# Two token tiles' last 64 inner values abreast on TensorE's row halves, in the down products of a shared FFN

## The chip, the cores and the metric

The kernel runs on one core of a Trainium2 chip. A core has five engines with queues of their own, which meet at semaphores: TensorE (matrix products; in the profile PE, its weight loads PEld), VectorE (DVE), ScalarE (ACT), GpSimd (POOL) and SyncE (SP, which here issues most DMA transfers). Products land in PSUM; everything else lives in SBUF or, off the core, in HBM. The metric is the device time of one execution in microseconds, and smaller is better.

## The reference, cut to what matters

The kernel computes one layer: cross attention, then a mixture of 64 experts with six of them per token, and a shared FFN that every token passes. The change touches the shared FFN. B, S, D = 4, 512, 512 give 2048 tokens; the shared FFN has FS = 704 inner values.

```python
def _shared_swiglu(x, wg, wu, wd):
    return jax.nn.silu(x @ wg.T) * (x @ wu.T) @ wd.T
...
g = jnp.einsum('ecd,efd->ecf', buf, w_gate)
u = jnp.einsum('ecd,efd->ecf', buf, w_up)
eo = jnp.einsum('ecf,edf->ecd', jax.nn.silu(g) * u, w_down)
gathered = eo[se, pos_c] * (sw * valid.astype(sw.dtype))[:, None]
y = jnp.zeros_like(x).at[st].add(gathered).reshape(B, S, D)
return y + _shared_swiglu(hidden_states, sh_gate, sh_up, sh_down)
```

## The kernel before

All arrays are float32. The tokens form 16 tiles of 128 (`TB` = 4 tiles in each of the 4 batches), and `acc` holds for each tile the residual to which everything is added.

The order of the work: attention over all tiles with the router, which scatters token numbers into lists in HBM (`list_d`, line 477); near its end, the shared FFN of batch 0, interleaved with the last tiles' routing and with `plan()`, which loads the lists back (line 491), sums them on VectorE (line 504), spreads them (508), turns them on TensorE (515) and writes `lists` (518). Then come the gate and up products of batch 1, whose down products wait; the loop over 64 experts (gather tokens, line 834; products, lines 871 to 927; results to `eo_d`, lines 952 and 956); and the tail: the down products of batch 1, the whole shared FFN of batches 2 and 3, and, interleaved with them, 96 gathers of expert results by GpSimd (line 1017), each followed by a weighted sum into `acc` on VectorE (line 1028). A tile whose last sum is done is written out (line 1005).

The order on each engine is written out by hand inside `manual_schedule`: an engine runs its instructions in the order in which the Python code issues them, and generators with `yield` interleave the parts. In `shared(b, get)`:

- The inner values come in six chunks, `FSC`: five of 128 and one of 64. For each, line 132 makes the gate and up products of all 512 tokens, line 143 the silu on ScalarE and line 144 the multiplication into `hid` on VectorE. In the last chunk gate and up share one product: gate in rows 0 to 63 of the PSUM bank, up in rows 64 to 127.
- The down products (lines 146 to 153): for each tile m one PSUM bank from `get.pd()`, six products accumulated in it (the last with 64 rows), and one addition into `acc` (line 152). A float32 product shows in the trace as two passes, each with a weight load of its own.
- Where PSUM comes from: for batch 0, `Here.pd` takes a tile of the pool `ps_s` (line 758), which has two buffers, shared with `Here.pair`; for batches 1 to 3, `There.pd` rotates over four banks, `pd0, ph, pd1, pt` (line 801).
- For batch 0, lines 776 to 778 issue before each tile m a step of `plan()`, so that on VectorE the list work stands between the additions:

```python
for n_lists in (1, 1, 0, 1):
    advance(lists_made, n_lists)
    next(work)
```

- In the tail, `slices()` (lines 1033 to 1044) issues one part of the shared FFN at a time; after each, line 1054 lets a share of the weighted sums follow, all that are left from the first tile of batch 3 on. `added(t)` counts a tile's contributions.
- `load_shared()` (line 110) loads the weights during the last attention tiles; line 120 loads the last 64 rows of the down weights.

Of the kernel before, what the change touches and what calls it, by code (L numbers as in the profile page):

```python
# [12 lines left out]
ALU = mybir.AluOpType  # L13
AX = mybir.AxisListType

P = 128
# [6 lines left out]
TB = S // P  # L23
# [7 lines left out]
FS = 704  # L31
FC = [(0, 128), (128, 128), (256, 96)]
FSC = [(i * P, min(P, FS - i * P)) for i in range((FS + P - 1) // P)]
# [3 lines left out]
HALF = P // 2  # L37
# [4 lines left out]
def xattn_moe_kernel(ctx, tc, a, out):  # L42
    nc = tc.nc
# [10 lines left out]
    acc = keep.tile([P, NT, D], F32, name="acc")  # L54
# [44 lines left out]
    def slab(*shape):  # L99
        n = 1  # L100
        for m in shape:
            n *= m
        names = "abc"[:len(shape)]
        return slabs.tile([P, NC * D], F32, tag="slab", name="slab")[:, :n].rearrange(
            f"p ({' '.join(names)}) -> p {' '.join(names)}", **dict(zip(names, shape)))


    sh_gu, sh_down = [], []

    def load_shared():  # L110
        for c in range(NC):
            sh_gu.append(slab(2 * FS))
            nc.sync.dma_start(sh_gu[-1], a["sh_guT"][c * P:(c + 1) * P, :])
        for f in range(0, len(FSC), 3):
            sh_down.append(slab(3, D))
            full = min(3, FS // P - f)
            nc.sync.dma_start(sh_down[-1][:, :full, :],
                              a["sh_downT"][f * P:(f + full) * P, :].rearrange("(c p) n -> p c n", p=P))
            if full < 3:
                nc.sync.dma_start(sh_down[-1][:FS % P, full, :], a["sh_downT"][(f + full) * P:, :])  # L120

    def shared(b, get):


        xT = slab(NC, S)
        nc.sync.dma_start(xT, h2T_d.rearrange("(c p) n -> p c n", p=P)[:, :, b * S:(b + 1) * S])
        yield
        hid = [get.hid() for _ in range(0, len(FSC), 3)]

        def product(dst, w0):  # L130
            for c in range(NC):
                nc.tensor.matmul(dst, sh_gu[c][:, w0:w0 + P], xT[:, c, :], start=c == 0, stop=c == NC - 1)  # L132

        for fc, (f0, fn) in enumerate(FSC):
            pg, pu = get.pair()
            product(pg, f0)
            if fn == P:
                product(pu, FS + FS % P + f0)
            else:
                pu = pg[fn:]  # L140
            yield
            sg = get.sg()
            nc.scalar.activation(sg[:fn], pg[:fn], AF.Silu)
            nc.vector.tensor_tensor(hid[fc // 3][:fn, fc % 3, :], sg[:fn], pu[:fn], ALU.mult)
            yield
        for m in range(TB):
            pd = get.pd()
            for fc, (f0, fn) in enumerate(FSC):
                nc.tensor.matmul(pd, hid[fc // 3][:fn, fc % 3, m * P:(m + 1) * P], sh_down[fc // 3][:fn, fc % 3, :],
                                 start=fc == 0, stop=fc == len(FSC) - 1)  # L150
            t = b * TB + m
            nc.vector.tensor_tensor(acc[:, t, :], pd, acc[:, t, :], ALU.add)
            yield

    swp = ctx.enter_context(tc.tile_pool(name="swp", bufs=1))
# [4 lines left out]
    with ExitStack() as att:  # L160
# [14 lines left out]
        rows = {n: wts.tile([P, 1, D], F32, name=n) for n in ("bq", "bo")}  # L175
# [411 lines left out]
        with tc.manual_schedule(engines=engines):  # L587
# [83 lines left out]
            m = B * DCA  # L671
# [43 lines left out]
            for u, (t, g) in enumerate(units):  # L715
                b, i = divmod(t, TB)
                pd, rd, sm = tail[t]
# [34 lines left out]
            class Here:  # L752
                hid = staticmethod(lambda: w2.tile([P, NC, SC], F32, tag="pr", name="pr")[:, :3, :])
                sg = staticmethod(lambda: w2.tile([P, NC, P], F32, tag="pT", name="pT", bufs=5).rearrange(
                    "p a b -> p (a b)"))
                pair = staticmethod(lambda: (lambda ps: (ps[:, 0, :], ps[:, 1, :]))(
                    ps_s.tile([P, 2, SC], F32, tag="ps", name="ps")))
                pd = staticmethod(lambda: ps_s.tile([P, 2, SC], F32, tag="ps", name="ps")[:, 0, :])
# [20 lines left out]
            for steps in (oldest, older, newer, lists_made, work):  # L779
# [8 lines left out]
    pa, ph, pg, pu, pl, pt, pd0, pd1 = (psum.tile([P, 512], F32, name=n)  # L788
                                        for n in ("pa", "ph", "pg", "pu", "pl", "pt", "pd0", "pd1"))
# [4 lines left out]
    class Late:  # L794
        hid = staticmethod(lambda: latep.tile([P, 3, S], F32, tag="hid", name="hid"))
        sg = staticmethod(lambda: There.sg())
        pair = staticmethod(lambda: There.pair())
        pd = staticmethod(lambda: There.pd())

    class There:  # L800
        pairs, pds = [(pg, pu), (pa, pl)], [pd0, ph, pd1, pt]
        hid = staticmethod(lambda: m2.tile([P, CT, D], F32, tag="eo", name="eo"))
        sg = staticmethod(lambda: m2.tile([P, 512], F32, tag="sg", name="sg"))
# [23 lines left out]
    def tokens(e):  # L827

        xg = m2.tile([P, 2 * CT, D // 2], F32, tag="xg", name="xg")
        if e < 2:  # L830
            nc.gpsimd.memset(xg, 0.0)
        for k in range(2 * CT):
            at = e * 2 * CT + k
            nc.gpsimd.indirect_dma_start(  # L834
                out=xg[:, k, :], out_offset=None, in_=h2_d.rearrange("t (h n) -> (t h) n", h=2),
                in_offset=bass.IndirectOffsetOnAxis(ap=lists[:, at:at + 1], axis=0),
                bounds_check=2 * B * S - 1, oob_is_err=False)
        return xg
# [137 lines left out]
    with tc.manual_schedule(engines=engines | {mybir.EngineType.SP}):  # L976
        for e in range(E):
            wgu, xT_e = held, xT
            hid = m2.tile([P, len(FC), CAP], F32, tag="ehid", name="ehid")
            uh = gate_up_first(hid, wgu, xT_e, kinds[e])  # L980
            if e + 2 < E:
                xg[e + 2] = tokens(e + 2)
            if e + 1 < E:
                xT = turned_tokens(xg.pop(e + 1))
            next(rest, None)
            gate_up_second(hid, wgu, xT_e, uh, kinds[e])
            next(rest, None)
            held = up.pop(e + 1, None)
            if e + 2 < E:
                up[e + 2] = up_weights(e + 2)  # L990
            next(rest, None)
            rest = down(e, hid, wd, kinds[e])
            if e + 1 < E:
                wd = down_weights(e + 1)
        for _ in rest:
            pass

        left = {t: TOPK + (t >= TB) for t in range(NT)}  # L1000

        def added(t):
            left[t] -= 1
            if not left[t]:
                nc.sync.dma_start(out[t * P:(t + 1) * P, :], acc[:, t, :])


        places = []
        for _ in range(2):
            x = m2.tile([P, 2 * CT, D // 2], F32, tag="xg", name="xg").rearrange("p k n -> p (k n)")  # L1010
            w = ewp.tile([P, NC, 2 * F], F32, tag="wgu", name="wgu").rearrange("p c f -> p (c f)")
            places += [y[:, i * D:(i + 1) * D] for y, n in ((x, CT), (w, NC * 2 * F // D)) for i in range(n)]
        gathered = []

        def gather(t, k):
            g = places[len(gathered) % len(places)]
            nc.gpsimd.indirect_dma_start(
                out=g, out_offset=None, in_=eo_d[:, :],
                in_offset=bass.IndirectOffsetOnAxis(ap=slot_get[:, t, k:k + 1], axis=0))
            gathered.append((t, k, g))  # L1020

        def combine(rows):
            ready = iter(rows)
            for i in range(len(rows)):
                while len(gathered) < min(i + len(places), len(rows)):
                    gather(*next(ready))
                t, k, g = gathered[i]
                nc.vector.scalar_tensor_tensor(acc[:, t, :], g, top_w[:, t, k:k + 1], acc[:, t, :],
                                               ALU.mult, ALU.add)
                added(t)  # L1030
                yield

        def slices():
            for m in range(TB):
                next(others[1])
                added(TB + m)
                yield
            for b in range(2, B):
                for n, _ in enumerate(others[b]):
                    if n >= 2 * len(FSC):  # L1040
                        added(b * TB + n - 2 * len(FSC))
                    elif n % 2 == 0:
                        continue
                    yield

        def tiles_of(b):
            return list(range(b * TB, (b + 1) * TB))

        sums = combine([(t, k) for b in (0, 2, 1, 3) for t in tiles_of(b) for k in range(TOPK)])
        last = TB + 2 * (len(FSC) + TB) - 3  # L1050
        behind = len(places) - 2
        done = 0
        for step, _ in enumerate(slices(), 1):
            while done < (NT * TOPK * step // last - behind if step < last else NT * TOPK):
                next(sums)
                done += 1
# [53 lines left out]
```

## Time and profile before

| what | us |
|---|---|
| median of 3 runs | 1739.08 (1729.93 to 1741.41) |
| the profiled execution | 1736.63 |
| its span, first to last instruction | 1734.5 |
| TensorE busy (mean granted clock 0.992) | 1643.8 |
| VectorE busy | 966.4 |
| GpSimd busy | 835.0 |
| ScalarE busy | 584.9 |

All that follows of the profile is of this one execution; the times are from the span's start. The stages, by the busy time of their engines:

| stage | from, to (us) | TensorE | VectorE | GpSimd |
|---|---|---|---|---|
| gate and up of batch 0, last routing | 597, 643 | 44.31 | 14.03 | 12.32 |
| down of batch 0, lists | 643, 668 | 23.25 | 10.83 | 6.48 |
| gate and up of batch 1 | 668, 707 | 37.99 | 9.02 | 20.12 |
| experts | 707, 1578 | 844.92 | 417.36 | 369.84 |
| tail, first part | 1578, 1661 | 82.47 | 41.73 | 56.54 |
| tail, second part | 1661, 1734 | 62.25 | 44.26 | 47.29 |

A line of a timeline reads: start, length, engine, source line, operation, written tile <- read tiles, shapes, count; in square brackets how long the engine had been idle and what ended that. Of TensorE's products the ends are modelled: consecutive ones overlap in the records, so the distance from start to start tells what one costs.

### The profile page before, as it was taken

Reading aid. Unit: us, or ns where it says so; the run is one execution under the profiler, and the core shown is the slowest. Engines: PE = TensorE matmul, PEld = TensorE weight load, DVE = VectorE, ACT = ScalarE, POOL = GpSimd, SP = SyncE. Lnnn points to the kernel's source line nnn. Section 1 sums busy time; section 2 is a strip of 40 time slices with the busy share of each in tenths; the row PEclk is TensorE's granted clock in tenths of the full one; section 3 lists DMA queues with packets and bytes.
Section 4 is the critical chain, followed back from the end, with each engine's and each line's share of the span. In section 5 each row is a group of like instructions: output and inputs, shape, how many; then the busy total and the mean of one; then the engine's idle time right before and its main releaser. Section 6 shows DMA issues by size and latency. Waiting matters only on the chain.

```text
span 1734.5 us, 27121 instructions
## 1 busy us (share of the span) xinstructions
PE 1643.8 (95%) x9906; PEld 1052.2 (61%) x9906; DVE 966.4 (56%) x1722; ACT 584.9 (34%) x1313; POOL 835.0 (48%) x783
## 2 busy tenths in 40 slices
PE   8899999999988899999999999999999999999998
PEld 5455555555555444666766777776677776674433
DVE  5577777777777533344444554554545544442647
ACT  3565565555656410122222222222222222121000
POOL 5346466665554325244444454444444444413675
PEclk9999999999999999999999999999999999999998
DMA  8000110010201113467766787777778777665675
GB/s 276 22 22 26 35 29 19 20 48 25 88 20 35 62 38 125 146 219 250 242 232 221 259 277 253 253 263 269 243 261 283 242 269 233 214 208 165 192 219 175
DMA packets 127702, 280.98 MB, mean 162 GB/s; under 512 B 26029, under 2 KB 54741, under 8 KB 119137
## 3 DMA queue, kind: packets, MB, share of 16 engines
q1 hardware_dynamic: 97984, 226.85, 38.0%
q0 software_dynamic: 29184, 50.52, 10.3%
q8 instruction: 195, 3.19, 0.7%
q14 instruction: 51, 0.41, 0.1%
q10 hardware_dynamic: 288, 0.01, 0.0%
HBM read 238.69 MB, written 63.55 MB: 174 GB/s over the span
## 4 chain that ended last, share of the span: by engine, by line
PE 79%; DVE 12%; issue 3%; ACT 2%; another core or an unknown queue 2%; DMA 1%; POOL 1%; SPq 0%; DVEq 0%; POOLq 0%; ACTq 0%
PE pa L871 10%; PE pd L921 10%; PE mm L282 8%; PE pd L927 7%; PE pg L871 5%; PE pu L871 5%; PE pl L871 5%; PE x L376 4%; DVE nm L357 4%; PE ph L883 3%; PE pc L387 3%; PE ps L351 3%; PE ps L132 2%; PE pg L132 2%
## 5 line engine op out<-in xcount | busy, mean ns | idle before, releaser
L834 POOL DMA_INDIRECT xg<-h_d,lists x384 | 387.9, 1010 | 478.0 <-DVE xT L846 377.5
L846 DVE STREAM_TRANSPOSE xT<-xg 64x768 f32<-64x768 f32 x256 | 248.5, 971 | 16.2 <-DMA xg<-h_d,lists 11.2
L921 PE MATMUL pd<-wd,ehid 128*128 128x512 f32 (+1 forms) x384 | 203.7, 625 | 5.1 <-issue 5.1
L871 PEld LDWEIGHTS pa<-xT,wgu 128*128 128x128 f32 x1024 | 174.5, 190 | 43.6 <-issue 27.7
L871 PE MATMUL pa<-xT,wgu 128*128 128x192 f32 (+3 forms) x1024 | 188.3, 337 | 6.7 <-ACT eo L955 2.9
L888 DVE TENSOR_TENSOR ehid<-sg,pa 128x256 f32<-128x256 f32 x64 | 26.9, 421 | 273.6 <-ACT sg L887 167.7
L361 ACT ACTIVATE pr<-ps,nm 128x496 f32<-128x496 f32 x256 | 170.9, 676 | 8.5 <-DVE nm L357 7.9
L376 PEld LDWEIGHTS x<-ident,pr 128*128 128x128 f32 x1024 | 114.0, 142 | 92.9 <-issue 60.0
L381 ACT COPY pT<-x 128x512 f32<-128x512 f32 x192 | 106.6, 585 | 188.2 <-PE x L376 185.8
L376 PE MATMUL x<-ident,pr 128*128 128x128 f32 x1024 | 143.5, 281 | 15.3 <-ACT slab L276 7.6
L357 DVE TENSOR_REDUCE nm<-ps 128x2 f32<-128x992 f32 x128 | 145.0, 1173 | 12.3 <-PE ps L351 12.2
L265 POOL TENSOR_TENSOR hn_r<-hn_var,mhalf 128x16 f32<-128x16 f32 (+1 forms) x33 | 97.5, 2956 | 106.0 <-DVE hn_var L263 93.4
L927 PE MATMUL pd<-wd,ehid 128*64 128x256 f32 x1092 | 138.1, 385 | 8.7 <-issue 5.2
L871 PEld LDWEIGHTS pg<-xT,wgu 128*128 128x128 f32 x544 | 92.6, 190 | 38.9 <-issue 34.6
L927 PEld LDWEIGHTS pd<-wd,ehid 128*64 128x64 f32 x1092 | 76.8, 138 | 63.5 <-issue 30.2
L477 POOL DMA_INDIRECT list_d<-token_id,r_put x96 | 97.7, 1018 | 27.4 <-issue 25.0
L871 PE MATMUL pg<-xT,wgu 128*128 128x192 f32 (+5 forms) x544 | 107.3, 340 | 3.3 <-issue 3.3
L871 PE MATMUL pu<-xT,wgu 128*128 128x192 f32 (+5 forms) x544 | 107.1, 339 | 0.9 <-issue 0.9
L871 PE MATMUL pl<-xT,wgu 128*128 128x192 f32 (+4 forms) x512 | 102.4, 343 | 0.0
L907 ACT ACTIVATE sg<-pg 128x512 f32<-128x512 f32 x64 | 38.2, 597 | 184.8 <-PE pg L871 175.5
L871 PEld LDWEIGHTS pu<-xT,wgu 128*128 128x128 f32 x544 | 91.6, 190 | 7.0 <-issue 1.3
L871 PEld LDWEIGHTS pl<-xT,wgu 128*128 128x128 f32 x512 | 87.6, 190 | 5.7
(222 smaller groups left out, 2399.4 us busy)
## 6 DMA issues: line engine op xcount, KB each, us to landing
wgu<-in_w_gu SPq DMA_DIRECT2D x64, 1408.0 KB
wd<-in_w_down SPq DMA_DIRECT2D x64, 512.0 KB
eo_d<-eo SPq DMA_DIRECT2D x64, 512.0 KB
eo_d<-eo SPq DMA_DIRECT2D x128, 128.0 KB
wd<-in_w_down SPq DMA_DIRECT2D x64, 192.0 KB
xg<-h_d,lists POOLq DMA_INDIRECT x384
xT<-in_xT SPq DMA_DIRECT2D x16, 256.0 KB
acc<-in_x SPq DMA_DIRECT2D x16, 256.0 KB
```

Source lines behind the costliest of these rows:

```text
L265: nc.gpsimd.tensor_tensor(r[:m], var[:m], mhalf[:m], ALU.pow)
L282: nc.tensor.matmul(ps[:m], lT[:, c, :], w[:, c, :], start=c == 0, stop=c == n - 1)
L357: nc.vector.tensor_reduce(nm[:, 2 * i:2 * i + 2], pss[i][:, :, :SM], AX.X, ALU.max, negate=True)
L361: nc.scalar.activation(pr[:, r, :SM], pss[i][:, r % 2, :SM], AF.Exp, bias=nm[:, r:r + 1], accum_out=sm[:, g * NC + r:g * NC + r + 1])
L376: nc.tensor.transpose(tp[:, r, :], pr[:, r, c * P:(c + 1) * P], ident)
L381: (engine.copy if engine is nc.scalar else engine.tensor_copy)(pT, tp)
L477: nc.gpsimd.indirect_dma_start(out=list_d[k][:, :], out_offset=bass.IndirectOffsetOnAxis(ap=put[:, k:k + 1], axis=0), in_=token_id[:, t:t ...
L834: nc.gpsimd.indirect_dma_start(out=xg[:, k, :], out_offset=None, in_=h2_d.rearrange("t (h n) -> (t h) n", h=2), in_offset=bass.IndirectOff ...
L846: nc.vector.transpose(xT[s * half:(s + 1) * half].rearrange("p c (k a i) -> p k c a i", a=2, i=Q)[:, :, :, a, :], xg[a * half:(a + 1) * ha ...
L871: nc.tensor.matmul(dst, wgu[:, c, w0:w0 + P], xT[:, c, lo:hi], start=c == 0, stop=c == NC - 1)
L921: nc.tensor.matmul(pd, hid[:fn, fc, m * P:(m + 1) * P], wd[:fn, fc, :], start=fc == 0, stop=fc == len(FC) - 1)
L927: nc.tensor.matmul(pd[d * HALF:(d + 1) * HALF, i * D // 2:(i + 1) * D // 2], hid[:fn, fc, P + i * HALF:P + (i + 1) * HALF], wd[:fn, fc, d ...
```

## The change

The down products go by two tiles. Each tile of a pair gets its PSUM bank and its five full products; after the second tile's five, the 64-row product of the first tile runs on rows 0 to 63 of TensorE and that of the second on rows 64 to 127. For this the last 64 rows of the down weights are loaded twice, to both halves of the partitions, and the last chunk of `hid` is written by two multiplications: the even tiles' tokens to partitions 0 to 63, the odd tiles' to 64 to 127. The two additions into `acc` follow the pair. The generator still yields once per tile, and the counts of `added` follow the additions.

```diff
             if full < 3:
-                nc.sync.dma_start(sh_down[-1][:FS % P, full, :], a["sh_downT"][(f + full) * P:, :])
+                for h in range(2):
+                    nc.sync.dma_start(sh_down[-1][h * HALF:(h + 1) * HALF, full, :], a["sh_downT"][(f + full) * P:, :])
...
             nc.scalar.activation(sg[:fn], pg[:fn], AF.Silu)
-            nc.vector.tensor_tensor(hid[fc // 3][:fn, fc % 3, :], sg[:fn], pu[:fn], ALU.mult)
-            yield
+            if fn == P:
+                nc.vector.tensor_tensor(hid[fc // 3][:, fc % 3, :], sg, pu, ALU.mult)
+            else:
+                by_tile = [v.rearrange("p (k h n) -> p k h n", h=2, n=P) for v in (hid[fc // 3][:, fc % 3, :], sg, pu)]
+                for h in range(2):
+                    nc.vector.tensor_tensor(by_tile[0][h * HALF:(h + 1) * HALF, :, h, :], by_tile[1][:fn, :, h, :],
+                                            by_tile[2][:fn, :, h, :], ALU.mult)
+            yield
+        pds = []
         for m in range(TB):
-            pd = get.pd()
-            for fc, (f0, fn) in enumerate(FSC):
-                nc.tensor.matmul(pd, hid[fc // 3][:fn, fc % 3, m * P:(m + 1) * P], sh_down[fc // 3][:fn, fc % 3, :],
-                                 start=fc == 0, stop=fc == len(FSC) - 1)
-            t = b * TB + m
-            nc.vector.tensor_tensor(acc[:, t, :], pd, acc[:, t, :], ALU.add)
+            pds.append(get.pd())
+            for fc in range(len(FSC) - 1):
+                nc.tensor.matmul(pds[-1], hid[fc // 3][:, fc % 3, m * P:(m + 1) * P], sh_down[fc // 3][:, fc % 3, :],
+                                 start=fc == 0, stop=False)
+            if m % 2:
+                fc = len(FSC) - 1
+                for h in range(2):
+                    rows, cols = slice(h * HALF, (h + 1) * HALF), slice((m - 1 + h) * P, (m + h) * P)
+                    nc.tensor.matmul(pds[h], hid[fc // 3][rows, fc % 3, cols], sh_down[fc // 3][rows, fc % 3, :],
+                                     start=False, stop=True)
+                for h in range(2):
+                    t = b * TB + m - 1 + h
+                    nc.vector.tensor_tensor(acc[:, t, :], pds[h], acc[:, t, :], ALU.add)
+                pds.clear()
             yield
...
         def slices():
             for m in range(TB):
                 next(others[1])
-                added(TB + m)
+                for t in range(m - 1, m + 1) if m % 2 else ():
+                    added(TB + t)
                 yield
             for b in range(2, B):
                 for n, _ in enumerate(others[b]):
                     if n >= 2 * len(FSC):
-                        added(b * TB + n - 2 * len(FSC))
+                        m = n - 2 * len(FSC)
+                        for t in range(m - 1, m + 1) if m % 2 else ():
+                            added(b * TB + t)
```

## The prediction

> **What bounds the kernel now.** I read the page's chain of waits first, then the timelines of the four places where the changed code runs: 643–668 us (batch 0) and, after the experts, 1578–1601, 1639–1661 and 1706–1729 us (batches 1, 2, 3).
>
> ```profile
> PE 79%; DVE 12%; issue 3%; ACT 2%; another core or an unknown queue 2%; DMA 1%; POOL 1%; SPq 0%; DVEq 0%; POOLq 0%; ACTq 0%
> ```
> TensorE carries four fifths of the chain, so a microsecond won or lost on it in front of the experts arrives at the end. The weight loads of one token tile (start, length, engine, line, shape, idle before) give the price of the part that changes:
>
> ```profile
> 652.34 0.19 PEld L149 LDWEIGHTS ps<-slab,pr 128*128 128x128 f32 x1 [0.24 <-issue]
> 653.28 0.29 PEld L149 LDWEIGHTS ps<-slab,pr 64*128 64x128 f32 x2 [0.76 <-issue]
> 654.34 0.30 PEld L149 LDWEIGHTS ps<-slab,pr 128*128 128x128 f32 x2 [0.76 <-issue]
> ```
> A product takes two passes, a full pass 0.43 us (eight of line 132 in 3.43), so twelve would be 5.15; tiles follow each other in 5.54 (648.80 to 654.34). The missing 0.39 is the two changes of row count, seen as 0.76 of idle for 0.24. The last 64 values cost 0.86 + 0.39 = 1.25 us per tile.
>
> The stage of batch 0, TensorE and then VectorE:
>
> ```profile
> 643.30 16.65 PE L149 MATMUL ps<-slab,pr 128*128 128x512 f32 x36
> 660.78 0.68 PE L515 MATMUL x<-ident,pT 128*128 128x128 f32 x4 [0.83 <-DVE pT L508]
> 661.56 5.61 PE L149 MATMUL ps<-slab,pr 128*128 128x512 f32 x12
> 667.95 1.56 PE L132 MATMUL pg<-slab 128*128 128x512 f32 x3 [0.78 <-DVE acc L152]
> ```
> ```profile
> 648.90 0.69 DVE L152 TENSOR_TENSOR acc<-ps,acc 128x512 f32<-128x512 f32 x1 [1.80 <-PE ps L149]
> 655.85 1.48 DVE L504 TENSOR_REDUCE pT<-li 128x128 f32<-128x768 int32 x1 [6.26 <-DMA li<-list_d]
> 658.91 1.46 DVE L504 TENSOR_REDUCE pT<-li 64x128 f32<-64x768 int32 x1 [1.58 <-DMA li<-list_d]
> 660.29 0.61 DVE L508 TENSOR_SCALAR pT<-pT 128x128 f32<-128x128 f32 x4
> 660.83 1.27 DVE L152 TENSOR_TENSOR acc<-ps,acc 128x512 f32<-128x512 f32 x2
> ...
> 667.21 0.69 DVE L152 TENSOR_TENSOR acc<-ps,acc 128x512 f32<-128x512 f32 x1 [4.05 <-PE ps L149]
> ```
> VectorE adds tile 0 at 648.90, then sits in its queue on the expert lists, which land at 655.85 and 658.91; only at 660.83 come the adds of tiles 1 and 2. The products have two PSUM buffers: tile 2 takes the one that tile 0's early add freed, and tile 3 can start only when tile 1's add ends (661.5): its first product is at 661.56. That date is set by the lists, not by TensorE.
>
> The tail, GpSimd's gathers and VectorE's last work (lines of the gathers with idle, then the end):
>
> ```profile
> 1613.86 1.34 POOL L1017 DMA_INDIRECT wgu<-eo_d,slot_get  x1 [5.58 <-DVE acc L1028]
> ...
> 1695.33 1.21 POOL L1017 DMA_INDIRECT wgu<-eo_d,slot_get  x1 [5.18 <-DVE acc L1028]
> ...
> 1725.29 0.94 POOL L1017 DMA_INDIRECT wgu<-eo_d,slot_get  x1 [0.30 <-DVE acc L1028]
> ```
> ```profile
> 1728.81 0.75 DVE L1028 SCALAR_TENSOR_TENSOR acc<-wgu,top_w,acc 128x512 f32<-128x512 f32 x1 [0.62 <-DMA wgu<-eo_d,slot_get]
> 1729.48 0.68 DVE L152 TENSOR_TENSOR acc<-ph,acc 128x512 f32<-128x512 f32 x1
> 1730.08 0.68 DVE L152 TENSOR_TENSOR acc<-pd,acc 128x512 f32<-128x512 f32 x1
> 1730.68 0.68 DVE L152 TENSOR_TENSOR acc<-pt,acc 128x512 f32<-128x512 f32 x1
> ```
> TensorE ends at 1728.62 (1723.01 and 5.61), the last gathered sum at 1729.56: two chains that tie. The gathers have only two long gaps, each because a weighted sum stood on VectorE behind a product of the shared FFN.
>
> **The change, part by part.**
>
> *The pair.* Two tiles: 11.08 us before. After: twenty full passes, 8.59, and one 64-row part for both if the halves run abreast. No row shows 64-row halves; the nearest is four 32-row products of the scores:
>
> ```profile
> 305.09 1.11 PE L351 MATMUL ps<-slab,qT 32*128 32x496 f32 x8
> 306.14 0.33 PE L376 MATMUL x<-ident,pr 128*128 128x128 f32 x1
> ```
> Eight passes of 496 columns would be 3.3 us one behind the other; the next work starts after 1.05. They overlap, so I take 1.25 for the pair: 9.84, a saving of 1.25. Bound on the other side: not abreast, 1.72 + 0.39, a saving of only 0.39. Eight pairs: at most 10 us of TensorE's work, 2.5 in batch 0 and 7.5 in the tail.
>
> *Batch 0: the saving turns into a wait.* Both PSUM buffers are held until the pair's last product. Tiles 0 and 1: 643.30 + 8.59 + 1.25 = 653.1. Their adds are now issued in the step of tile 1, behind the two list reductions in VectorE's order; tile 0's early add at 648.90 is gone. So tile 2 waits for the lists as tile 3 did: 661.56, and 0.15 later for the split multiplication (below). TensorE is idle from 653.1 to 661.7, 8.6 us. Queued behind it: tile 2, the list transposes, tile 3, the whole of batch 1's gate and up products, GpSimd's clearing of xg (which waited for these products until 667.37) and SP's first expert weights (667.25). From 661.71: tile 2's five products 4.29, the four transposes 0.7 (they were in the old wait; 660.78 with 0.68), then tile 3 to the next product as before, 667.95 − 661.56 = 6.39, and 0.6 because two adds now stand before the freed bank (1.27 for two, 0.69 for one). Batch 1 starts at 673.7 instead of 667.95: **+5.75**.
>
> The rule against this change stands in the Trainium skill, TensorEngine Tiling, "Gotcha 1: PSUM Pressure": row tiles write to different banks, so packing rows raises the demand for PSUM. Without it this stage would be −2.5; with two buffers, as the rows show them, it is +5.75. In the tail four banks rotate and a pair leaves two free, so there I charge nothing for it.
>
> *The clock.* TensorE idled 5.38 us once, at 1688.36, and the granted clock shows the price:
>
> ```profile
> 1688.40:1693.70 5.30, 0.00 (x0) 0.00 (x0) 0.00 (x0) 0.61 (x2) 1.45 (x2) 0.81 0.50 149
> 1693.70:1698.50 4.80, 4.76 (x6) 2.18 (x7) 4.71 (x7) 0.47 (x1) 2.56 (x3) 0.50 0.32 108
> ```
> (The third number from the end is the clock.) After the restart it was 0.50 for 4.8 us: 2.4 lost. The skill's TensorE: Matmul & The Clock Gate, Part 1, has the full clock back after one busy window of about 3.4 us, an estimate of 1.7 lost. The sum of the stage is 7.45 by the rule, 8.15 by the row; I take the row: **+2.4**. Upper end: two windows at half, 3.4.
>
> *The split multiplication.* 64x512 in 0.69 becomes two of 64x256; the nearest row is 128x256 in 0.421, so +0.15 (lower end 0). In batch 0 it stands ahead of the list chain and is counted; in the tail the pair needs it 4.3 us later than the tile did: nothing.
>
> *The second load of the 64 rows* adds 128 KB and one issue of 0.54 us on SP (line 120, 527.70), whose next transfer is at 550.79; first use after 650. Nothing. No other transfer is moved; GpSimd's order is unchanged.
>
> *The tail.* TensorE's 7.5 us alone buy 0.9, since the gathers end the kernel. They win only as far as their two gaps shrink: the first ends with a product of batch 2 that follows one saved batch (2.5), the second follows two (5.0). If the signals move with TensorE's products, −5.0; if they don't, 0. At the very end, tile 0's add of batch 3 (1712.04 before) goes behind the last sum too: four adds, +0.6. Between −4.4 and +0.6 I take **−3.5**, near the first, as those gaps begin and end with TensorE's products.
>
> Sum: 5.75 + 2.4 − 3.5 = **+4.65 us** (the 0.15 is inside 5.75). The profiled execution took 1736.63 (span 1734.5), so 1741.3 like for like; it lies 2.45 below the median of the three runs. I predict at the median: 1739.08 + 4.65, **1743.7**.
>
> **Rivals.**
>
> *Faster: the gathers lose both gaps whole.* Both (5.58 + 5.18 = 10.8) end with late signals to ScalarE; the page puts them down to an unknown queue. If TensorE's lead removes both, the tail gives −10.8 + 0.6 = −10.2, against +8.15: −2.0, 1737. It decides where the gathers gain over 8.8. For it: the run of 1729.93. Against: nothing shows the cause. Chance 0.2.
>
> *The halves run one behind the other.* Batch 0 +0.86; the tail's gaps shrink by at most 1.55, less 0.6 for the add: +8.1, 1747. Against: the scores' rows. Chance 0.1.
>
> *The wait is smaller or larger.* Lists landing 8 us earlier would leave no wait; they hang on six scatters from 645.41 and twelve loads to 656.7 that the change doesn't touch. 0.05 for a gain there, 0.05 for a longer loss (clock 3.4, the experts' loop thrown out of step).
>
> *My forecast*, slower by 1 to 9 us: 0.6.
>
> **Range and chances.** The bounds: 5.6 + 1.7 − 10.2 = −3 and 6.6 + 3.4 + 0.6 = +10.6, on 1739: 1736 to 1750; the runs of before spread from 1730 to 1741, so I take 1734 to 1751. One per cent (17 us, about what a measurement of this kernel tells from no change) is beyond every case: faster by over 1% 0.02, slower 0.06, within 0.92.
>
> **What would show it.** Right: TensorE idle for some 8 us before the third tile of batch 0, released by an add of VectorE after the lists; PEclk at 0.5 after it; batch 1's first product near 673.7; tail pairs every 9.8 us with both halves' loads starting together; four adds after the last sum. Wrong: tile 2 starting near 653, tail pairs of 10.7, or gathers without gaps and an end before 1730.

## The result, and the profile after

The changed kernel takes 1745.9 us (median of 22 runs, 1742.16 to 1754.56). The kernel before, run between them on the same chip, takes 1738.85 (22 runs). The ratio is 1.0042, 95% interval 1.0027 to 1.0057: slower by 7 us (4.7 to 9.9), which is under half a per cent. The forecast was 1743.7, +4.65. The profiled execution has a span of 1748.4.

In the page of after, the chain of waits shows that TensorE's share hardly moved (78% for 79%); the 2% of the unknown queue are gone from it, and "issue", DMA and GpSimd have one per cent more each:

```profile
PE 78%; DVE 11%; issue 4%; ACT 2%; POOL 2%; DMA 2%; another core or an unknown queue 0%; SPq 0%; DVEq 0%; POOLq 0%
```

Batch 0's down products in the timeline of TensorE, after (start, length, engine, line, operation, tiles, shapes, count, idle before):

```profile
644.82 8.80 PE L158 MATMUL ps<-slab,pr 128*128 128x512 f32 x20
653.55 1.13 PE L164 MATMUL ps<-slab,pr 64*128 64x512 f32 x4
663.48 6.84 PE L158 MATMUL ps<-slab,pr 128*128 128x512 f32 x10 [8.80 <-DVE acc L168]
670.16 0.65 PE L532 MATMUL x<-ident,pT 128*128 128x128 f32 x4
670.74 4.56 PE L158 MATMUL ps<-slab,pr 128*128 128x512 f32 x10
...
677.73 3.70 PE L134 MATMUL pg<-slab 128*128 128x512 f32 x8 [1.38 <-DVE acc L168]
```

Twenty full passes, then the pair of 64-row products in 1.13, then nothing for 8.80 us. The third tile's ten passes take 6.84 where the fourth's take 4.56, so 2.3 us are lost there. What it waited for stands in VectorE's timeline of after:

```profile
657.58 1.45 DVE L521 TENSOR_REDUCE pT<-li 128x128 f32<-128x768 int32 x1 [8.67 <-DMA li<-list_d]
660.85 1.44 DVE L521 TENSOR_REDUCE pT<-li 64x128 f32<-64x768 int32 x1 [1.83 <-DMA li<-list_d]
662.21 0.61 DVE L525 TENSOR_SCALAR pT<-pT 128x128 f32<-128x128 f32 x4
662.75 1.27 DVE L168 TENSOR_TENSOR acc<-ps,acc 128x512 f32<-128x512 f32 x2
```

The additions that free both banks stand behind the two reductions of the lists, which wait for DMA. No early addition is left; the one at 648.90 of before has no counterpart.

Why the restart is slow is in the windows of after (from and to, length, busy time and count of TensorE's products, its weight loads, VectorE, ScalarE, GpSimd; then the granted clock, 1.00 ahead of the wait and 0.50 behind it, the DMA share, GB/s):

```profile
644.80:653.50 8.70, 8.70 (x22) 3.69 (x21) 3.74 (x16) 0.00 (x0) 4.88 (x5) 1.00 0.46 142
...
663.40:666.60 3.20, 3.12 (x4) 1.50 (x5) 0.62 (x2) 0.00 (x0) 0.00 (x0) 0.50 0.00 0
```

Stages by the trace, each from the start of one product to that of the next named one:

| stage (us) | before | after | change |
|---|---|---|---|
| first down product of batch 0 to first gate product of batch 1 | 24.65 | 32.91 | +8.26 |
| from there to the first expert | 39.49 | 39.66 | +0.17 |
| the experts | 871.09 | 875.78 | +4.69 |
| tail: first down product of batch 1 to the end | 156.0 | 155.28 | −0.72 |
| of the tail, to TensorE's last product | 150.1 | 143.74 | −6.36 |

The experts' stage is not the change's doing: this is one profile each, and it reads 870 to 881 across the profiles below, in kernels of either kind (887 in e8, where the first expert starts inside batch 1's products). What lies ahead of the first down product, where only the second load of the 64 rows is new, also differs by 1.5. The medians leave about −1.2 for everything but batch 0 (7.05 − 8.26).

The tail, TensorE in after:

```profile
1593.17 4.56 PE L158 MATMUL pd<-slab,hid 128*128 128x512 f32 x10 [0.72 <-ACT eo L972]
1597.56 4.45 PE L158 MATMUL ph<-slab,hid 128*128 128x512 f32 x10
1601.95 0.69 PE L164 MATMUL pd<-slab,hid 64*128 64x512 f32 x1
1601.95 0.69 PE L164 MATMUL ph<-slab,hid 64*128 64x512 f32 x1
...
1603.01 4.56 PE L158 MATMUL pd<-slab,hid 128*128 128x512 f32 x10
```

The two halves start in the same hundredth of a microsecond, and a pair takes 9.84 (1593.17 to 1603.01). The saving is there. But GpSimd's gathers (after; idle before in brackets) still have both gaps:

```profile
1597.85 0.96 POOL L1034 DMA_INDIRECT xg<-eo_d,slot_get  x1 [47.27 <-DMA eo_d<-eo]
...
1627.85 1.33 POOL L1034 DMA_INDIRECT wgu<-eo_d,slot_get  x1 [4.78 <-DVE acc L1045]
...
1708.94 1.21 POOL L1034 DMA_INDIRECT wgu<-eo_d,slot_get  x1 [4.85 <-DVE acc L1045]
```

They were 5.58 and 5.18. The last gather starts 140.2 us after the first; in before it was 142.0. And VectorE ends with the last gathered row, then four additions, where before had three. TensorE's last product had ended at 1736.91, 5.9 us ahead of the first of them:

```profile
1742.04 0.75 DVE L1045 SCALAR_TENSOR_TENSOR acc<-wgu,top_w,acc 128x512 f32<-128x512 f32 x1 [0.75 <-DMA wgu<-eo_d,slot_get]
1742.82 0.69 DVE L168 TENSOR_TENSOR acc<-pd,acc 128x512 f32<-128x512 f32 x1
...
1744.62 0.68 DVE L168 TENSOR_TENSOR acc<-pt,acc 128x512 f32<-128x512 f32 x1
```

### The profile page after: what moved, and what is told of

Its sections match the earlier page's. It is cut to its first block, busy times and chain, and to the rows that moved or that the text cites. A ratio compares the mean times of both kernels' runs of the same rounds, so it can differ in the third digit from the quotient of the medians.

```text
span 1748.4 us, 27121 instructions
## 1 busy us (share of the span) xinstructions
PE 1641.2 (94%) x9906; PEld 1053.9 (60%) x9906; DVE 966.9 (55%) x1726; ACT 586.0 (34%) x1313; POOL 835.3 (48%) x783
## 4 chain that ended last, share of the span: by engine, by line
PE 78%; DVE 11%; issue 4%; ACT 2%; POOL 2%; DMA 2%; another core or an unknown queue 0%; SPq 0%; DVEq 0%; POOLq 0%
PE pd L938 10%; PE pa L888 10%; PE mm L299 8%; PE pd L944 7%; PE pg L888 6%; PE pu L888 5%; PE pl L888 5%; PE x L393 4%; DVE nm L374 4%; PE ph L900 3%; PE pc L404 3%; PE ps L368 2%; PE ps L134 2%; PE x L257 2%; PE pg L134 1%
## 5 line engine op out<-in xcount | busy, mean ns | idle before, releaser
L888 PEld LDWEIGHTS pa<-xT,wgu 128*128 128x128 f32 x1024 | 174.2, 190 | 44.3 <-issue 28.3
L938 PEld LDWEIGHTS pd<-wd,ehid 128*128 128x128 f32 (+1 forms) x384 | 62.0, 191 | 51.5 <-issue 48.2
```

The source lines that it names most:

```text
L888: nc.tensor.matmul(dst, wgu[:, c, w0:w0 + P], xT[:, c, lo:hi], start=c == 0, stop=c == NC - 1)
L938: nc.tensor.matmul(pd, hid[:fn, fc, m * P:(m + 1) * P], wd[:fn, fc, :], start=fc == 0, stop=fc == len(FC) - 1)
```

## The experiments

Times are set against the kernel before on the same chip. The chips differ: before took 1724.2 with e1 to e4, 1723.4 with e5 to e8, 1738.7 with e9 and e10, and 1734.8 with e11 and e12.

### Which stage carries the loss: e1 and e2

e1 pairs only in the tail, e2 only in batch 0; the other batches keep the old loop.

```diff
-            if fn == P:
+            if fn == P or b == 0:          (e2: b > 0, here and below)
...
+        for m in range(TB if b == 0 else 0):
+            (the old loop: six products, one addition, one yield)
-        for m in range(TB):
+        for m in range(0 if b == 0 else TB):
```

> Pairs in batches 1 to 3 only; batch 0 goes tile by tile as before. Wait theory (batch 0's two PSUM buffers cost about 8 us, the tail gives about 1): 0 to 2 us below before, batch 1's first product at the same 24.7 us after batch 0's first down product as before, tail's down products 9.84 us a pair, and the end still set by the gathers. Rival (the pairs themselves or their later additions cost time): above before by 3 us or more, as the changed kernel is.

> Pairs in batch 0 only; batches 1 to 3 tile by tile as before. Wait theory: 8 us above before, all of it between batch 0's first down product and batch 1's first gate product (about 32.9 us instead of 24.7, with TensorE idle for 8.8 of them and half clock behind it). Rival (the loss lies in the tail or in the experts): within 2 us of before.

e1: 1723.62 against 1724.2, ratio 0.9993 (0.9973 to 1.0013). e2: 1732.93, 1.0052 (1.0032 to 1.0073), that is +8.7 (5.5 to 12.6); its batch 0 takes 33.6 us. So the loss comes from batch 0, and the tail gives nothing that this measurement sees. The two profiles show why. In e1 the stage from the tail's first product to TensorE's last takes 134.64, in e2, whose tail is the old one, 142.1: TensorE gains 7.46, the 7.5 of the sum. The whole tail takes 147.36 and 148.06. TensorE's last product of e1, and VectorE's last work:

```profile
1709.61 0.59 PE L172 MATMUL pt<-slab,eo 64*128 64x512 f32 x1
```
```profile
1716.51 0.75 DVE L1053 SCALAR_TENSOR_TENSOR acc<-wgu,top_w,acc 128x512 f32<-128x512 f32 x1 [0.74 <-DMA wgu<-eo_d,slot_get]
1717.30 0.69 DVE L176 TENSOR_TENSOR acc<-pd,acc 128x512 f32<-128x512 f32 x1
```

TensorE is done at 1710.2; the end waits for a gathered row at 1716.5. In e2 the two chains tie: TensorE is done at 1729.08, the last gathered sum starts at 1729.40. On this chip the gathers have none of the 5 us gaps in e1 and only idles of up to 1.6 in e2, and still they leave the pairs nothing to win.

### The wait itself: e3, e4, e8

e3 leaves the pairs and issues the first pair's additions ahead of the second list reduction instead of behind it.

```diff
-            for n_lists in (1, 1, 0, 1):
+            for n_lists in (1, 0, 1, 1):
```

> The changed kernel, with the step of the plan that reduces the lists on VectorE issued after the first pair's additions instead of before them; nothing else moves. Wait theory: the third tile starts when the first addition ends, about 1.4 us after the pair instead of 8.8; the list transposes then wait for the lists ahead of the fourth tile; batch 1 starts some 8 us earlier than in the changed kernel and the clock stays full: 8 us below the changed kernel, that is from 2 below to 1 above before. Rival (the third tile waits for the lists or for PSUM whatever VectorE's order is): as the changed kernel, 7 above before.

1726.77, ratio 1.0017 (1.0001 to 1.0033): some 5 us of the loss gone with one step moved, though not down to the 2 below to 1 above that were expected. TensorE in e3:

```profile
646.27 1.13 PE L164 MATMUL ps<-slab,pr 64*128 64x512 f32 x4
648.18 4.56 PE L158 MATMUL ps<-slab,pr 128*128 128x512 f32 x10 [0.78 <-DVE acc L168]
655.83 0.68 PE L532 MATMUL x<-ident,pT 128*128 128x128 f32 x4 [3.09 <-DVE pT L525]
656.43 6.26 PE L158 MATMUL ps<-slab,pr 128*128 128x512 f32 x10
```

The third tile starts 0.78 after the pair, released by the addition. A smaller wait takes the old one's place: the list transposes stand between tiles three and four in TensorE's order and wait 3.09 for the lists, and the fourth tile runs part of its passes at half clock (6.26 us; the granted clock is 0.50 from 657.0 to 660.3). Batch 0 takes 27.58, against 24.65 before.

e4 gives each pair the two banks of one PSUM buffer, so that a pair holds one buffer of the two, and puts the list transposes behind the last pair.

```diff
-                pd = staticmethod(lambda: ps_s.tile([P, 2, SC], F32, tag="ps", name="ps")[:, 0, :])
+                banks = []
...
+                def pd(cls):
+                    if not cls.banks:
+                        ps = ps_s.tile([P, 2, SC], F32, tag="ps", name="ps")
+                        cls.banks = [ps[:, 0, :], ps[:, 1, :]]
+                    return cls.banks.pop(0)
-            for n_lists in (1, 1, 0, 1):
+            for n_lists in (1, 1, 0, 0):
...
+            advance(lists_made, 1)
```

> The changed kernel, with each pair of batch 0 in the two banks of one PSUM buffer (a buffer has two, one was left unused), and the list transposes issued after the fourth tile. Wait theory: no product of batch 0 waits for a buffer or for the lists; four tiles in 19.7 us without a gap, batch 1's first product about 21.5 us after batch 0's first down product (24.7 before, 32.9 in the changed kernel): 3 us below before from batch 0, and with the tail 3 to 5 below before. Rival (batch 1 then waits for the lists or the transposes instead): within 1 us of before.

1721.44, ratio 0.9986 (0.9974 to 0.9998), 2.8 below the kernel before by the medians, just short of what was expected. TensorE in e4, then VectorE's turning of the lists:

```profile
646.89 1.13 PE L164 MATMUL ps<-slab,pr 64*128 64x512 f32 x4
647.95 8.85 PE L158 MATMUL ps<-slab,pr 128*128 128x512 f32 x20
656.73 1.13 PE L164 MATMUL ps<-slab,pr 64*128 64x512 f32 x4
657.79 0.70 PE L532 MATMUL x<-ident,pT 128*128 128x128 f32 x4
660.36 5.37 PE L134 MATMUL pg<-slab 128*128 128x512 f32 x8 [1.86 <-issue]
```
```profile
659.70 0.56 DVE L535 SCALAR_TENSOR_TENSOR lists<-x,none 128x384 int32<-128x384 f32 x1
```

Tile three follows the pair at once. Batch 0 takes 22.2; the pairs' 2.5 us are kept. The banks and the later transposes were not tried apart. What is left is 1.86 idle before batch 1, and its first product at 5.37 for 3.70 (granted clock 0.50), so that the next stage takes 41.32 where before has 39.49: three quarters of the stage's gain of 2.45 are given back there.

e8 tried to have that too: batch 1 begins in another bank pair, and the list transposes go in front of the last pair.

```diff
+                if b == 0 and m == TB - 1:
+                    get.lists()
...
+            Here.lists = staticmethod(lambda: advance(lists_made, 1))
...
-        pairs, pds = [(pg, pu), (pa, pl)], [pd0, ph, pd1, pt]
+        pairs, pds = [(pa, pl), (pg, pu)], [pd0, ph, pd1, pt]
```

> The changed kernel with each pair of batch 0 in the two banks of one PSUM buffer, the list transposes between the last tile's five products and its pair, and the gate and up products of the later batches starting in the other pair of banks (pa and pl before pg and pu), so that batch 1 does not wait for the last additions and the first expert does not wait for the last silu. Theory: batch 1's first product about 20.5 us after batch 0's first down product (24.7 before), no half clock behind it, the first expert 38.0 us after that (39.5 before): 5 to 6 us below before, with the tail's 0.6 among them. Rival (another wait takes the place, the lists or the weights of the first expert): 1 to 3 below before, as with the transposes last.

1721.5 against 1723.41, ratio 0.998 (0.9954 to 1.0006): 1.9 below by the medians, not the 5 to 6 of the theory but what the rival said, with an interval that covers no change. TensorE in e8, then VectorE's last two additions of batch 0:

```profile
661.70 3.67 PE L134 MATMUL pa<-slab 128*128 128x512 f32 x8 [1.57 <-issue]
...
692.67 1.02 PE L134 MATMUL pl<-slab 128*128 128x512 f32 x2
693.53 2.86 PE L898 MATMUL pa<-xT,wgu 128*128 128x192 f32 x16
697.12 2.84 PE L134 MATMUL pl<-slab 128*128 128x512 f32 x6
```
```profile
660.32 1.28 DVE L170 TENSOR_TENSOR acc<-ps,acc 128x512 f32<-128x512 f32 x2
```

An idle of 1.57 stands before batch 1 whatever its bank, so the bank was not its cause. The trace names no releaser here ("issue"), but all 14 profiles show the same: batch 1's first product starts 0.05 to 0.10 us after VectorE's last reading of batch 0's PSUM has ended. In before, after and here that is an addition (here until 661.60, the product at 661.70), in e4 the turning of the lists, line 535 (until 660.26, the product at 660.36). Batch 1's banks come from another pool, opened where the earlier ones end, which fits a batch that cannot start before the earlier banks are read out; no run takes this wait away. And this part of the order is not written out by hand: the first expert's products now run in the middle of a product of batch 1.

### The clock: e5

e5 is the changed kernel with nine wide products that nobody reads, issued ahead of the third tile, in the idle time.

```diff
+                get.fill()
...
+                    spare = wide_bank()
+                    for _ in range(9):
+                        nc.tensor.matmul(spare, sh_gu[0][:, :P], sh_gu[0][:, :512], start=True, stop=True)
```

> The changed kernel, with nine 128x512 products into an unused PSUM bank issued ahead of the third tile of batch 0 (7.7 us of extra work whose result nobody reads), so that TensorE works where it had waited. Theory of two prices (5.75 us of wait, 2.4 us of half clock behind it): the granted clock stays 1.0, the third tile's ten passes take 4.3 to 4.4 us instead of 6.84, batch 1 starts 30.5 us after batch 0's first down product instead of 32.9, and the time is 2.4 below the changed kernel, some 4 to 6 above before. Rival (the slow third tile has another cause): 32.9 and no change, or worse by the extra work.

TensorE in e5:

```profile
647.44 7.99 PE L782 MATMUL mm<-slab 128*128 128x512 f32 x18
656.74 4.56 PE L160 MATMUL ps<-slab,pr 128*128 128x512 f32 x10 [1.31 <-DVE acc L170]
```

The wait is as long as before, now filled, the granted clock stays at 1.00, and the third tile takes 4.56 where it took 6.84; batch 0 takes 31.06 for 32.91. This gain of 1.9 to 2.3 is seen in the trace alone. The time, 1732.4 (1.0046, 1.0027 to 1.0065), is 9 above before by the medians where 4 to 6 were expected, and can't tell 2 us from e2's or the changed kernel's loss.

### What holds the tail: e6, e7, e9, e10

e6 is the kernel before, e7 is e1, both with four of each token's six expert rows gathered and added.

```diff
-        left = {t: TOPK + (t >= TB) for t in range(NT)}
+        FEW = 4
+        left = {t: FEW + (t >= TB) for t in range(NT)}
...
-            while done < (NT * TOPK * step // last - behind if step < last else NT * TOPK):
+            while done < (NT * FEW * step // last - behind if step < last else NT * FEW):
```

> The kernel before with four of the six expert results gathered and summed per token (64 gathers instead of 96; the last two of each token are left out). Theory (with all six, the gathers end the tail): now TensorE ends it; the tail lasts TensorE's 142.1 us and about 4 behind them, 146, some 2 below before. Rival (the gathers are not the bound): as before within 1 us.

> The same, four of six gathered, with pairs in batches 1 to 3 (batch 0 tile by tile). Theory: with the gathers out of the way, the pairs earn nearly what they take off TensorE, 7.5 less 0.6 for one more addition at the end: about 7 below the kernel with four gathers and no pairs, where with six gathers they earned 0.6. Rival (pairs earn nothing for another reason, such as their later additions): within 2 us of the kernel with four gathers and no pairs.

e6: 1722.49; e7: 1714.6, a ratio of 0.9938 (0.9914 to 0.9963) to the kernel before. With a third fewer gathers the kernel before takes the same time as whole (0.9999, 0.9982 to 1.0017), which alone would fit the rival as well; but the pairs are now worth 7.9 us, where with all six they were worth 0.6. The tail takes 145.9 and 139.0, and VectorE's last addition in e6 waits for TensorE:

```profile
1714.80 0.69 DVE L152 TENSOR_TENSOR acc<-pt,acc 128x512 f32<-128x512 f32 x1 [1.19 <-PE pt L149]
```

So with six gathers two chains tie within 2 to 3 us in the kernel before (148.06 in e2, 145.9 here), and a shorter TensorE chain can only bring those. This pair of runs was made where the gathers have no gaps; it was not repeated on a chip where they have them.

e9 and e10 keep the last six weighted sums back until after the last pair's additions (e9 on e4, e10 on the kernel before), so that the additions don't come last.

```diff
-            while done < (NT * TOPK * step // last - behind if step < last else NT * TOPK):
+            while done < (NT * TOPK * step // last - behind if step < last else NT * TOPK - (6 if step < last + 3 else 0)):
```

> The kernel with each pair of batch 0 in the two banks of one PSUM buffer and the list transposes last, and now with the last six weighted sums issued behind the four last additions of the shared FFN instead of ahead of them. Theory (the gathers end the tail and TensorE leads by 8 us or more with pairs): the four additions go into VectorE's waits for gathers; the tail is some 1.8 to 2.4 us shorter (147.2 becomes 145), the time 4 to 6 below before. Rival (the additions then hold up the sums): the tail is as long or longer, the time 3 below before or less.

> The kernel before, tile by tile, with the last six weighted sums issued behind the last three additions. Theory (without pairs TensorE's last product, 142.1 us into the tail, comes just ahead of the last gather): the six sums wait for TensorE and run one behind the other after it, 1 to 4 us above before. Rival (the order of the last additions alone is worth something, without pairs too): 1 to 2 us below before.

e9: 1736.75 against 1738.66, 0.9986 (0.9966 to 1.0007), where 4 to 6 below were expected: a miss. The additions do go first, and what follows is bound by the gathers all the same. VectorE in e9:

```profile
1727.18 0.68 DVE L168 TENSOR_TENSOR acc<-pt,acc 128x512 f32<-128x512 f32 x1
...
1732.39 1.54 DVE L1053 SCALAR_TENSOR_TENSOR acc<-wgu,top_w,acc 128x512 f32<-128x512 f32 x2 [1.38 <-DMA wgu<-eo_d,slot_get]
```

e10: 1737.07, 0.9989 (0.9971 to 1.0008), where 1 to 4 above were expected. Its profile shows the expected wait for TensorE:

```profile
1737.70 0.69 DVE L152 TENSOR_TENSOR acc<-pt,acc 128x512 f32<-128x512 f32 x1 [4.75 <-PE pt L149]
```

but a tail longer by 2.5 in one profile beside a time lower by 1.6, with an interval that covers zero, tells nothing apart. On this chip both profiles have the two 5 us gaps, at 25 and 107 to 111 us after the first gather.

### What sets the gaps: e11 and e12

A gap of the gathers ends when VectorE gets on, and VectorE then stands on a multiplication, or waits for a silu, whose product TensorE had finished long before. VectorE in after, then ScalarE (`remote`: the profile names no releaser):

```profile
1626.23 0.69 DVE L147 TENSOR_TENSOR eo<-sg,pu 128x512 f32<-128x512 f32 x1 [8.97 <-remote]
...
1707.32 0.69 DVE L147 TENSOR_TENSOR eo<-sg,pu 128x512 f32<-128x512 f32 x1 [15.30 <-remote]
```
```profile
1697.39 0.60 ACT L145 ACTIVATE sg<-pg 128x512 f32<-128x512 f32 x1 [13.58 <-remote]
```

ScalarE in before, and VectorE in e1, on a chip without gaps, at the multiplication that stands at 1626.23 in after:

```profile
1693.09 0.60 ACT L143 ACTIVATE sg<-pg 128x512 f32<-128x512 f32 x1 [21.26 <-remote]
```
```profile
1602.46 0.69 DVE L147 TENSOR_TENSOR eo<-sg,pu 128x512 f32<-128x512 f32 x1 [2.82 <-PE pu L134]
```

In before the product had ended at 1678.1, and the signals of four products that ended from 1678 to 1688 all arrive within 0.3 us from 1693.06 on. In e1 the signal comes within 0.1 us of the product's end. The waits that hold the gathers end 28.4 and 109.5 us after the first gather in after, 28.3 and 109.8 in before, although TensorE is 2.5 and then 5 us ahead in after. A single signal can get through late but during a run of gathers, as at 1697.39. Either the signals are late by something of their own, or they wait for the gathers. They do not wait for code: in after no packet of the instruction queues moves from 1592 to 1630 or from 1687.5 to 1708. More places for gathered rows tell this apart: GpSimd can then run on for twelve more gathers while VectorE waits. e11 does this on e4, e12 on the kernel before.

```diff
+        for _ in range(2):
+            x = m2.tile([P, NC, CAP], F32, tag="xT", name="xT").rearrange("p c n -> p (c n)")
+            w = ewp.tile([P, len(FC), D], F32, tag="wd", name="wd").rearrange("p c n -> p (c n)")
+            places += [y[:, i * D:(i + 1) * D] for y in (x, w) for i in range(3)]
...
-        behind = len(places) - 2
+        behind = 14
```

> The changed kernel with the two banks of e4 (all four tiles of batch 0 without a wait) and with 28 places for gathered rows in place of 16: the experts' down weights and turned tokens give twelve more. GpSimd's order and VectorE's order stay; a gather only finds its place free earlier, so that GpSimd need not wait for weighted sums that stand behind a late product. Theory one, the signals of TensorE come late by an amount that the gathers do not set: VectorE's wait of some 9 us stays, but GpSimd has work for 15 us more, both gaps of the gathers (4.8 and 4.9) are gone, the last gather lies 9 to 10 earlier, at about 141 us after the first, and the tail takes 146 to 148 in place of 155.3; the time is 8 to 11 below that of the kernel before. Theory two, the signals are held until the gathers in flight have landed: twelve more gathers in flight hold them 15 us longer, the wait of VectorE grows from 9 to about 24, the gaps of the gathers come back later, about 40 us after the first gather in place of 25, and the tail stays at 152 to 157. On a chip where the gathers have no gaps to begin with (before at 1724), both say: no gaps, tail 146 to 148, time about 3 below before, as e4.

> The kernel before with the same 28 places and nothing else. Theory one: the gaps (5.58 and 5.18) are gone, the gathers end at about 140 us after the first, and now TensorE, whose last product of the tail ends 150.1 us after the tail's start, sets the end with one or two additions behind it: tail 151 to 153 in place of 156.0, time 3 to 5 below the kernel before, so that the pairs are worth 5 to 6 us here. Theory two: the gaps come back later, tail 153 to 158, time within 2 of the kernel before. On a chip without gaps both say: time within 1.5 of before.

e11: 1751.94 against 1734.79, 1.0098 (1.0074 to 1.0122). e12: 1753.09, 1.0112 (1.0082 to 1.0143). Room made both kernels slower by one per cent, more than either theory had said. VectorE's, GpSimd's and TensorE's first late line in e11:

```profile
1625.12 0.69 DVE L147 TENSOR_TENSOR eo<-sg,pu 128x512 f32<-128x512 f32 x1 [22.04 <-remote]
```
```profile
1583.68 0.96 POOL L1046 DMA_INDIRECT xg<-eo_d,slot_get  x1 [47.29 <-DMA eo_d<-eo]
...
1626.73 1.34 POOL L1046 DMA_INDIRECT wgu<-eo_d,slot_get  x1 [2.83 <-DVE eo L147]
```
```profile
1625.86 5.68 PE L134 MATMUL pu<-slab 128*128 128x512 f32 x8 [9.76 <-DVE eo L147]
```

and in e12, VectorE:

```profile
1631.10 0.69 DVE L144 TENSOR_TENSOR eo<-sg,pu 128x512 f32<-128x512 f32 x1 [23.81 <-remote]
```

The gap, at 25.2 us after the first gather with 16 places, opens at 40.2 and 40.0 with 28; VectorE's wait grows from 8.97 (after) to 22.04 and ends 41.4 and 45.0 us after the first gather. So far that is the second theory: the signals come about when the run of gathers is over. The run's last packet had ended 0.5 to 1.1 us before in before and after and 2.5 before in e12; in e11 it ended 1.1 after. The time is not what that theory said, for the wait now spreads. TensorE fills all its banks and stops for 9.76, which at this gap it did not do with 16 places, and restarts at half clock (5.68 for 3.60). The tail takes 172.5 in e11 and 168.9 in e12, 17 and 13 more than in after and before: most of the loss lies there. The opposite step, fewer places and so shorter runs of gathers, is what these two suggest; it was not tried.

## Why the prediction came out as it did

*The pair: right.* 9.84 forecast, 9.84 measured; TensorE ended the tail's work 7.46 earlier (e1 against e2), 7.5 forecast. The halves do run abreast, so that rival falls.

*Batch 0, +5.75 and the clock, +2.4: right.* Together 8.15, measured 8.26. TensorE idles 8.80 (8.6 forecast), released by the additions behind the lists, and e3 and e4 show the cause: free a bank earlier, by order (e3) or by number of banks (e4, which also moves the transposes), and the wait goes. The third tile loses 6.84 − 4.56 = 2.3 to the clock, near the 2.4 of the trace's row and not 1.7, the estimate from the Trainium skill's TensorE: Matmul & The Clock Gate, Part 1; e5 takes most of that back by keeping TensorE busy. The size is in part luck. In after the granted clock stands at 0.50 from 657.9 to 668.1; that stretch began during the idle, and the restart at 663.48 met 4.6 us of it. In e2, after an idle of 9.13, it met 5.3 us, and the tile took 7.20: 2.6 lost. Batch 1's first product came at 677.7 for 673.7: 1.5 of this arose ahead of the changed code, 2.3 is the clock, which that date had not in it.

*The split multiplication and the second load: right.* The two halves take 0.86 for 0.69 in batch 0, +0.17 where 0.15 was forecast, and no wait in the trace points at either.

*The tail, −3.5: the term that was mis-sized.* It measured −0.7 in the profile and about −1.2 by the medians, and that is the 2.4 us by which the forecast was low. The working took the gaps of the gathers to "begin and end with TensorE's products" and so to shrink by TensorE's lead. They shrank by 0.8 and 0.3. The end of each gap is a signal of TensorE that arrives about when GpSimd's run of gathers has ended, 28 and 110 us after the first gather whether TensorE is ahead or not; e11 and e12, with a longer run, move the first date by 13 and 17 us (to 41.4 and 45.0). The prediction had noted those late signals and that nothing showed their cause, so to side with −5.0 rather than 0 was a guess. The +0.6 for the addition behind the last sum is in the trace: four additions, not three.

*The rival of lost gaps: fell.* Both gaps are there in after. Where a chip has none (e1), the pairs in the tail still gain nothing beyond the measurement, since the gathers themselves come last.

*The smaller or larger wait: neither.* TensorE's idle was 8.80, and the experts' stage stayed within its spread.

Open: why TensorE's signals are held late in a long run of gathers, and not while the gathers each wait for their place; and why the profiles on the chips at 1724 show no such hold. Of the 14 us between the chips, about 8 lie in the tail (156.0 in before, 148.06 in e2, whose tail is the same) and about 5 ahead of batch 0's first down product (643.3 and 638.0), before the first of these gathers; no run shows what makes them.

## What to carry to other kernels

Before two tiles are made to share a step, count the buffers that the step now holds and look what stands in front of the instruction that frees them: here a pair that saves 1.25 us held both buffers behind a DMA and cost 8, and two banks from one buffer, with the list transposes behind the last pair, turned that into a gain. Where two chains end together, a shorter one brings only the distance to the other: the pairs took 7.5 us off TensorE and 1 off the kernel. A deeper prefetch is not free either: with room for 28 gathered rows in place of 16, VectorE waited 22 us in place of 9 for the signals it needed, and the kernel lost one per cent.

## What was not expected of the hardware

On the chips where before takes 1735 to 1739, completion signals of TensorE reach VectorE and ScalarE late, mostly in a burst about when a run of indirect gathers ends: 28 us after the first gather with 16 places, 41 to 45 with 28, though the products had ended up to 20 us earlier. In e11 and e12 that came with a loss of one per cent. Half clock also followed idles far shorter than batch 0's: 3.09 us in e3 (ten passes in 6.26) and 1.86 in e4 (eight in 5.37 for 3.70), but not the 1.57 in e8 (eight in 3.67, granted clock 1.00). And two 64-row products on the two halves of the rows start within 0.01 us of each other, pass by pass.
